# Two-level products in source order on every engine, sums two steps ahead, norms and side jobs cut into parts

## Chip, cores and metric

One core of a Trainium2 chip runs the program. The metric is the device time of one execution in microseconds (us); the time before is 2263.17 us, the median of 3 runs (2262.73 to 2263.86).

## What is computed

All arrays are float32. x is 3327 x 512; adj is 3327 x 3327, padded to 26 tiles of 128 rows.

```python
h = relu(layernorm(x))
a = (h @ Wq.T + bq) @ (h @ Wk.T + bk).T / sqrt(512) + adj + adj
x1 = x + softmax(a) @ (h @ Wv.T + bv)               # layer 0
h1 = relu(layernorm(x1))
A2 = adj + I;  d = diagonal(A2) ** -0.5
temp = A2 @ h1 @ W.T
out = x1 + relu((d * A2 * d.T) @ temp)              # layer 1
```

Three products have a 3327 x 3327 matrix on the left: exp(scores) with h (called g0 here), A2 with h1 (g1), and A2 with the scaled temp (g2). They are the "two-level products".

## The kernel before

**Scores.** The first part projects h and makes the exponentials of the scores in 52 pairs of row tiles, in a scheme with seven products in place of eight. It ends with pair 51. Each pair stores its exponentials and their sums to DRAM (`pd`), and sums of the adjacency (`sumd`: S3, S1, S2, S4 of each tile, of which the scores write S3 and S1). The matmuls are on L435, the accumulation of the row totals on L483, its last matmul against a column of ones on L490 (`total`), the sum S4 on L472 (`s4`, into a two-slot tile `mid 12` that is allocated anew for every two pairs).

**Steps of a product.** Each g runs seven sub-products (ORDER = p5, p1, p6, p7, p2, p3, p4). Each of these runs over two column strips s (896 and 768 columns, so moving operands of 448 and 384) and in each strip over seven steps t: six steps of two row tiles and a last one, t = None, of one tile. Hence 14 steps a sub-product, 98 a g, 294 in all; `number_of(g, r, s, t)` counts them. A step loads its left tile (`left`, two DMAs into one of five slots of `a_ring`, L658, L661 or L665; where the tile lies on the diagonal a VectorE add, L668, puts in the 1), forms four sums on VectorE (`four_sums`, L171 to L173, into one of three slots of `o_ring3`), and multiplies (L744: seven products, two matmul instructions each, into seven PSUM banks). The step t = None multiplies without sums (L736: four products, into the banks of p2, p3, p4 and into p8's).

**Right sides.** `Right` holds the eight 128 x 128 blocks of one step's right side: rows of h, h1 or temp from DRAM (`rowd`, L685), sometimes with more rows in `r_ring`, then one to two subtractions or additions and `four_differences` (L177 to L180) in `make`. A right side is made once and used in both strips.

**Gather.** After t = None, `gather` takes the seven banks and p8 apart: a ScalarE copy (L778), eight VectorE operations that read PSUM (L779 to L788), and `settle`, which adds into the result tiles `cts` (L767 to L774; two operations of full width, for p7 six, for p5 and p1 none). The next step's matmuls reuse the banks one by one, p1, p6, p7, p5, p2, p3, p4.

**Between the steps.** A table `between` places further work after steps: loads and makes of right sides; `Job`s, which add two adjacency tiles to S1 in turn and so write S2 and S4 for g1 (L808 to L820); and, as soon as rows of a result are complete, `attend` (g0: four products against the weights on L827 into bank p8, VectorE operations L842 and L843, the layer norm, a ScalarE Relu L847 and stores of x1 and h1), `temp` (g1: the same matmuls, a ScalarE multiplication L854, a store) and `finish` (g2: transposes L866 into bank p8, ScalarE L868, VectorE L869, the store of the output). There are 26 rows of each. `attend` and `temp` do 17 in the last sub-products of their g and 9 in the first of the next (every second step from step 0 of it, so one of the nine falls behind a t = None); two steps of each g's last strip hold two rows. `finish` stays in g2.

**What sets the order.** The scheduler of the framework orders the instructions of each engine by itself and may put later ones earlier; each engine's queue then runs in the order so fixed. Only the scores are held to source order, by the helper `in_order`, which chains each named engine's instructions. In the products the source places load two and sums one step ahead of the multiplication.

Of the kernel before, what the change touches and what calls it, by code (L numbers as in the profile page):

```python
# [15 lines left out]
P = 128  # L16
# [28 lines left out]
def graph_layers_kernel(  # L45
# [142 lines left out]
    def norm(src):  # L188

        st = small.tile([P, 6], F32, name="st")  # L190
        nc.vector.bn_stats(st, src)
        mv = small.tile([P, 2], F32, name="mv")
        nc.vector.bn_aggr(mv, st)
        ve = small.tile([P, 1], F32, name="ve")
        nc.vector.tensor_scalar(ve, mv[:, 1:2], EPS, None, op0=ALU.add)
        rstd = small.tile([P, 1], F32, name="rstd")
        nc.gpsimd.tensor_tensor(rstd, ve, mhalf, op=ALU.pow)
        nb = small.tile([P, 1], F32, name="nb")
        nc.vector.scalar_tensor_tensor(nb, mv[:, 0:1], -1.0, rstd, op0=ALU.mult, op1=ALU.mult)
        return rstd, nb  # L200
# [102 lines left out]
    def h_transposed(k):  # L303

        a, n = PACKS[k]
        for _, i in (o for o in order if o[0] == k):
            xt = first.pop(i) if i in first else load_x(i)
            rstd, nb = norm(xt)
            ht = n_ring([P, D], "ht")
            nc.scalar.activation(ht, xt, AF.Relu, bias=nb, scale=rstd)  # L310
            nc.gpsimd.dma_start(rowd[0][i], ht)
            pt = tp_bank("tp").rearrange("p (c e) -> p c e", c=DC)
            for c in range(DC):
                nc.tensor.transpose(pt[:, c], ht[:, c * P : (c + 1) * P], ident)
            w = slice((i % HALF - a) * P, (i % HALF - a + 1) * P)
            if i < HALF:
                nc.scalar.copy(hp[k][:, 0:2, :, w], pt.rearrange("p (a c) e -> p a c e", a=2))
            else:
                nc.scalar.copy(hp[k][:, 2, :, w], pt[:, 2:4])
                nc.vector.tensor_add(hp[k][:, 3, :, w], hp[k][:, 2, :, w], pt[:, 0:2])  # L320
                nc.vector.tensor_add(hp[k][:, 5, :, w], hp[k][:, 0, :, w], pt[:, 0:2])
        nc.vector.tensor_add(hp[k][:, 4], hp[k][:, 3], hp[k][:, 0])
        nc.vector.tensor_add(hp[k][:, 6], hp[k][:, 1], hp[k][:, 4])
# [78 lines left out]
    class Pair:  # L402
# [65 lines left out]
        def s4(self):  # L468
            if self.t % 2 == 0:
                Pair.fours = mid(12, [P, 2, Q[0]], "s4")  # L470
            self.last = Pair.fours[:, self.t % 2, : self.wd]
            nc.vector.tensor_add(self.last, self.e[:, 1], self.g[1][:, 0])  # L472
            nc.gpsimd.dma_start(self.to(pd)[:, 6], self.last)  # L473
# [11 lines left out]
        def total(self, m):  # L485

            if self.t < HALF - 1:
                return
            acc, ps = Pair.acc, tp_bank("tot")
            nc.tensor.matmul(ps[:1, : self.wd], ones, acc[:, m], start=True, stop=True)  # L490
            if m == 0:
                Pair.second = ps
                return
            lower, upper = acc[:1, 0], acc[:1, 1]
            nc.vector.tensor_copy(upper, Pair.second[:1, : self.wd])
            nc.vector.tensor_sub(lower, ps[:1, : self.wd], upper)
            c0 = STRIPS[self.s] * P
            dst = totd[:, c0 : c0 + 2 * H[self.s]].rearrange("o (y w) -> o y w", y=2)
            nc.gpsimd.dma_start(dst[:, :, self.c : self.c + self.wd], acc[:1])


    pairs = {}
    steps = [(n, t) for n in range(len(groups)) for t in range(HALF)]
# [32 lines left out]
    with in_order(*(e.engine for e in (nc.vector, nc.tensor, nc.gpsimd, nc.sync))):  # L536
# [14 lines left out]
        for what in (*beside[5:], *beside_of(k + 1)):  # L551
            what()
    nc.sync.dma_start(tot, totd[0].rearrange("(i p) -> p i", p=P))
# [5 lines left out]
    def seven():  # L559
        return {r: bank(ROLE[r], r) for r in ("p1", "p6", "p7", "p5", "p2", "p3", "p4")}  # L560

    def judge():
# [16 lines left out]
        one = small.tile([1, 4], F32, name="one")  # L579
# [17 lines left out]

    def prepare():
        wv_w1.append(weights(wvT))
        nc.vector.reciprocal(rs, tot)  # L600
        LD = adjT.shape[1]
        dg = const.tile([P, NT], F32, name="dg")
        with nc.allow_non_contiguous_dma(reason="the diagonal, once"):
            nc.sync.dma_start(dg, bass.AP(tensor=adjT.tensor, offset=adjT.offset, ap=[[LD + 1, P], [P * (LD + 1), NT]]))
        mh = const.tile([P, NT], F32, name="mh")
        nc.vector.memset(mh, -0.5)
# [23 lines left out]
    b_ring = ring(*((half, k) for k in (0, 1, 2, 3, 8, 9, 10, 11)))  # L630
# [12 lines left out]
    job_ring = ring(*spare[3:], (half, 14))  # L643
# [103 lines left out]
    def gather(ct, r, s, ps):  # L747
# [41 lines left out]
        if r == "p4" and s == 1:  # L789
            settle(hi)  # L790
        else:
            settle(slice(0, hw))
# [6 lines left out]
    class Job:  # L799


        def __init__(self, s, j):
            self.s, self.j = s, j

        def load(self):
            s, j, w, c0 = self.s, self.j, H[self.s], STRIPS[self.s] * P
            self.s1, *self.a = (job_ring([P, H[0]], "job")[:, :w] for _ in range(3))
            nc.gpsimd.dma_start(self.s1, sumd[s][j][:, 1])  # L808
            for k in range(2):
                r0 = (k * HALF + j) * P  # L810
                nc.gpsimd.dma_start(self.a[k], adjT[r0 : r0 + P, c0 : c0 + w])

        def make(self):
            before = self.s1
            for k, a in enumerate(self.a):
                tc.keep_in_program_order(nc.vector.tensor_add(a, a, before))  # L816
                d = diagonal(a, (k * HALF + self.j) * P, STRIPS[self.s] * P)
                if d:
                    nc.vector.tensor_add(a[:, d[0]], a[:, d[0]], d[1])
                nc.gpsimd.dma_start(sumd[self.s][self.j][:, 2 + k], a)  # L820
                before = a
# [8 lines left out]
    attended = []  # L830

    def attend(i):

        if not attended:
            bv_sb = mid(12, [P, D], "bv_sb")
            nc.sync.dma_start(bv_sb, bass.AP(tensor=bv.tensor, offset=bv.offset, ap=[[0, P], [1, D]]))
            attended.append(bv_sb)
        xt = view(2, 1).rearrange("p a w -> p (a w)")[:, len(attended) % 3 * D :][:, :D]
        attended.append(i)
        nc.sync.dma_start(xt, x[i * P : (i + 1) * P])  # L840
        ps = times_weights(i, wv_w1[0])
        nc.vector.scalar_tensor_tensor(xt, ps, rs[:, i : i + 1], xt, op0=ALU.mult, op1=ALU.add)  # L842
        nc.vector.tensor_add(xt, xt, attended[0])  # L843
        nc.gpsimd.dma_start(x1d[i], xt)
        rstd, nb = norm(xt)
        h1 = h_ring([P, D], "h1")
        nc.scalar.activation(h1, xt, AF.Relu, bias=nb, scale=rstd)  # L847
        nc.gpsimd.dma_start(rowd[1][i], h1)

# [6 lines left out]

    def finish(i, z=(0, 1), spot=None):
# [4 lines left out]
        xr = (xr_ring if spot is None else xr_last)([P, D], "xr")  # L862
        nc.sync.dma_start(xr[:, c0:c1], x1d[i][:, c0:c1])
# [21 lines left out]
    for g in range(3):  # L885
        for n, r in enumerate(ORDER):
            for t, e in enumerate(every):
                k = number_of(g, n, 0, t)
                rh = rights[g, r, e]
                lead = 3 if n == 0 else 7  # L890
                for what, when in ((rh.load, k - lead), (rh.make, k - 2 if n == 0 else k - 4)):
# [5 lines left out]
    for g, what in ((0, attend), (1, temp), (2, finish)):  # L897
        for t, i in {2: 0, 3: 1, 4: 2, 5: 3}.items():
            at(number_of(g, 5, 1, t), what, i)
        for t, i in enumerate((4, 5, 6, 14, 15, 16)):  # L900
            at(number_of(g, 6, 0, t), what, i)
        for t, its in {1: (7,), 2: (8, 9), 3: (10,), 4: (11, 12), 5: (13,)}.items():
            for i in its:
                at(number_of(g, 6, 1, t), what, i)
        if g < 2:
            for k, i in enumerate((*range(20, 26), *range(17, 20))):
                at(number_of(g + 1, 0, 0, 0) + 2 * k, what, i)
    for t, i in enumerate((17, 18, 19)):
        at(number_of(2, 6, 1, t), finish, i)
    for t, i in enumerate(range(20, NT)):  # L910
        at(number_of(2, 4, 0, t), finish, i, (1,))
    at(number_of(0, 0, 0, 1), prepare)
    at(number_of(0, 0, 1, 1), judge)
    at(number_of(1, 1, 0, 4), other_weights)

    jobs = [Job(s, j) for s in range(2) for j in range(HALF)]
    k0, k1 = number_of(0, 0, 0, 4), number_of(1, 1, 1, 2)
    for n, job in enumerate(jobs):
        k = k0 + n * (k1 - k0) // len(jobs)
        at(k, job.load)  # L920
        at(k + 3, job.make)

    for k in range(2):
        steps[k].load()
    for what in early:
        what()
    steps[0].sums()
    for k, step in enumerate(steps):
        if k + 2 < len(steps):
            steps[k + 2].load()  # L930
        if k + 1 < len(steps):
            steps[k + 1].sums()
        if step.t == 0:
            ps = seven()
        if not cts:
            set_up()
        if step.t is None:
            ps["p8"] = bank(ROLE["p8"], "p8")
        step.multiply(ps)
        if step.t is None:  # L940
            gather(cts[step.s], step.r, step.s, ps)
        for what, args in between.get(k, ()):
            what(*args)
    for n, i in enumerate(range(20, NT)):
# [378 lines left out]
```

## Time and profile before

The profiled execution took 2255.93 us, its span is 2254.1 us.

| view | reading |
|---|---|
| profiled execution / span | 2255.93 us / 2254.1 us |
| median of the timed runs | 2263.17 us |
| VectorE busy in the span | 1587.6 us (70%), 3095 instructions |
| ScalarE busy | 231.8 us (10%), 336 instructions |
| GpSimd busy | 391.4 us (17%), 629 instructions |
| DMA, mean over the span | 254 GB/s, 572.58 MB |
| 14 matmuls L744 undisturbed (chain of work) | 5.26 us with 448 columns, 4.51 us with 384 |
| 8 matmuls L827 undisturbed (chain of work) | 3.43 us |
| left tiles, issue to landing, median | 3.5 to 6.3 us |
| rows for right sides, issue to landing, median | 3.9 and 4.3 us |

A busy time is the union of an engine's instructions; matmul records overlap, so their mean duration (514 ns on L744) is longer than their distance. The idle time behind the bar of a group is what the engine stood still directly before its instructions, with the instruction that ended it. "SPq" is the queue of SyncE, which issues DMAs in order and waits in front of one whose buffer is not free.

### The profile page before, as it was taken

Reading aid. Unit: us, or ns where it says so; the run is one execution under the profiler, and the core shown is the slowest. Engines: PE = TensorE matmul, PEld = TensorE weight load, DVE = VectorE, ACT = ScalarE, POOL = GpSimd, SP = SyncE. Lnnn points to the kernel's source line nnn. Section 1 sums busy time; section 2 is a strip of 40 time slices with the busy share of each in tenths; the row PEclk is TensorE's granted clock in tenths of the full one; section 3 lists DMA queues with packets and bytes.
Section 4 is the critical chain, followed back from the end, with each engine's and each line's share of the span. In section 5 each row is a group of like instructions: output and inputs, shape, how many; then the busy total and the mean of one; then the engine's idle time right before and its main releaser. Section 6 shows DMA issues by size and latency. Waiting matters only on the chain.

```text
span 2254.1 us, 20860 instructions
## 1 busy us (share of the span) xinstructions
PE 2185.9 (97%) x6252; PEld 1164.8 (52%) x6252; DVE 1587.6 (70%) x3095; ACT 231.8 (10%) x336; POOL 391.4 (17%) x629
## 2 busy tenths in 40 slices
PE   8999999999989998999989999999999999999997
PEld 5555555455545454554444455555545555555554
DVE  6369788788867667877666777777645447677675
ACT  5321211122100000000100000000000000000011
POOL 5233333333321111011232220000000000000001
PEclk9999999999999999999999999999999999999998
DMA  7568888889988889888687787666646558766685
GB/s 249 206 213 305 292 300 284 301 290 321 360 269 318 322 293 335 284 296 280 205 292 261 245 307 247 222 206 215 198 140 207 160 170 287 223 199 214 202 278 162
DMA packets 237546, 572.58 MB, mean 254 GB/s; under 512 B 34218, under 2 KB 105360, under 8 KB 237424
## 3 DMA queue, kind: packets, MB, share of 16 engines
q1 hardware_dynamic: 185344, 368.48, 50.8%
q0 software_dynamic: 51216, 201.11, 24.0%
q10 hardware_dynamic: 864, 1.57, 0.2%
q8 instruction: 51, 0.84, 0.2%
q14 instruction: 71, 0.58, 0.1%
HBM read 403.21 MB, written 167.85 MB: 253 GB/s over the span
## 4 chain that ended last, share of the span: by engine, by line
PE 64%; issue 16%; POOL 7%; DMA 7%; DVE 3%; ACT 0%; SPq 0%; POOLq 0%; DVEq 0%
PE p L744 46%; PE p L827 6%; PE p L736 4%; DMA sum<-job 2%; PE Y L435 2%; PE Y L334 1%; POOL p L462 1%; POOL p L466 1%; POOL p L443 1%; POOL sum L427 1%; DMA job<-in_adjT_dram 1%; POOL p L473 1%; PE Z L435 1%; DMA rows<-row 1%; PE mm L288 1%
## 5 line engine op out<-in xcount | busy, mean ns | idle before, releaser
L744 PE MATMUL p<-part,b 128*128 128x448 f32 (+1 forms) x3528 | 1257.6, 514 | 13.5 <-DVE part L779 6.1
L744 PEld LDWEIGHTS p<-part,b 128*128 128x128 f32 x3528 | 668.7, 190 | 582.5 <-issue 318.7
L171 DVE TENSOR_TENSOR part<-part 128x896 f32<-128x896 f32 (+1 forms) x252 | 257.2, 1021 | 204.0 <-PE p L744 119.8
L435 PE MATMUL Y<-qt,hp 128*128 128x448 f32 (+1 forms) x832 | 309.0, 514 | 2.6 <-DVE g L439 1.6
L435 PEld LDWEIGHTS Y<-qt,hp 128*128 128x128 f32 x832 | 157.4, 190 | 138.0 <-issue 72.3
L435 PE MATMUL Z<-qt,hp 128*128 128x384 f32 (+1 forms) x416 | 162.6, 513 | 0.0
L827 PE MATMUL p<-w,ct 128*128 128x512 f32 x272 | 130.0, 619 | 13.4 <-DVE part L842 13.4
L173 DVE TENSOR_TENSOR part<-part,part 128x448 f32<-128x448 f32 (+1 forms) x219 | 128.7, 588 | 12.7
L736 PE MATMUL p<-part,b 128*128 128x448 f32 (+1 forms) x336 | 125.0, 513 | 6.6 <-DVE part L842 3.4
L172 DVE TENSOR_TENSOR part<-part,part 128x448 f32<-128x448 f32 (+1 forms) x219 | 128.6, 587 | 3.6
L435 PEld LDWEIGHTS Z<-qt,hp 128*128 128x128 f32 x416 | 78.8, 190 | 67.4 <-issue 36.2
L439 DVE SCALAR_TENSOR_TENSOR g<-g,Y 128x384 f32<-128x384 f32 (+1 forms) x156 | 91.4, 586 | 26.9 <-PE Y L435 25.1
L855 POOL DMA_DIRECT2D row<-ts x26 | 14.1, 542 | 467.3 <-ACT ts L854 467.3
L736 PEld LDWEIGHTS p<-part,b 128*128 128x128 f32 x336 | 63.3, 190 | 61.5 <-issue 32.7
L827 PEld LDWEIGHTS p<-w,ct 128*128 128x128 f32 x272 | 53.7, 199 | 76.9 <-issue 54.1
L778 ACT COPY part<-p 128x384 f32<-128x384 f32 (+1 forms) x33 | 16.5, 501 | 686.0 <-PE p L744 685.9
L435 PE MATMUL X<-qt,hp 128*128 128x384 f32 (+1 forms) x208 | 81.1, 512 | 0.0
L442 ACT ACTIVATE g<-g 128x768 f32<-128x768 f32 (+1 forms) x48 | 43.0, 896 | 352.5 <-DVE g L439 301.8
L427 POOL DMA_DIRECT2D sum<-o x52 | 37.0, 711 | 217.3 <-DVE o L421 151.6
L89 POOL DMA_DIRECT2D out_dram<-r x34 | 18.4, 543 | 308.9 <-DVE r L869 304.5
L816 DVE TENSOR_TENSOR job<-job 128x896 f32<-128x896 f32 (+1 forms) x52 | 53.0, 1020 | 23.5 <-DMA job<-in_adjT_dram 23.3
L177 DVE TENSOR_TENSOR b<-b 128x128 f32<-128x128 f32 x126 | 36.1, 287 | 46.9 <-DMA b<-row 38.3
(159 smaller groups left out, 1911.3 us busy)
## 6 DMA issues: line engine op xcount, KB each, us to landing
part<-sum SPq DMA_DIRECT2D x104, 448.0 KB, 4.7
part<-p SPq DMA_DIRECT2D x91, 448.0 KB, 6.3
part<-sum SPq DMA_DIRECT2D x104, 384.0 KB, 3.5
part<-p SPq DMA_DIRECT2D x91, 384.0 KB, 4.3
part<-in_adjT_dram SPq DMA_DIRECT2D x78, 448.0 KB, 4.4
b<-row SPq DMA_DIRECT2D x234, 128.0 KB, 3.9
part<-in_adjT_dram SPq DMA_DIRECT2D x78, 384.0 KB, 3.7
g<-in_adjT_dram SPq DMA_DIRECT2D x52, 448.0 KB, 4.5
```

The lines of the kernel that those rows point to most:

```text
L171: nc.vector.tensor_add(o[:, 0:2], g[:, 0:4:3], g[:, 1:2].to_broadcast([P, 2, g.shape[-1]]))
L172: nc.vector.tensor_add(o[:, 2], o[:, 1], g[:, 0])
L173: nc.vector.tensor_add(o[:, 3], o[:, 2], g[:, 2])
L177: yield nc.vector.tensor_sub(b[4], b[0], b[1])
L427: nc.gpsimd.dma_start(self.to(sumd)[:, 0:2], self.o)
L435: nc.tensor.matmul(ps[:, :wd], h_of(self.t, name, k), qt[B[name]][:, k], start=start and k == 0, stop=k == 1, skip_group_check=True)
L439: nc.vector.scalar_tensor_tensor(a[n], a[n], 2.0, ps[:, :wd], op0=ALU.mult, op1=ALU.add if sign > 0 else ALU.subtract)
L442: nc.scalar.activation(g[1], g[1], AF.Exp, **({"bias": pad} if self.t == HALF - 1 else {}))
L736: nc.tensor.matmul(ps[("p2", "p3", "p4", "p8")[k]][:, :w], b[:, z], a[:, 0, y], start=k == 3, stop=True)
L744: nc.tensor.matmul(ps[r][:, :w], b[:, i], m, start=self.t == 0, stop=self.t == PAIRS - 1 and r in ("p1", "p5", "p6", "p7"))
L816: tc.keep_in_program_order(nc.vector.tensor_add(a, a, before))
L827: nc.tensor.matmul(ps, cts[s][y][d][:, k * P : (k + 1) * P], w[d], start=d == 0, stop=d == DC - 1)
```

## The change

1. **Order.** All steps before the last strip of the last sub-product (`last = number_of(2, 6, 1, 0)`) are traced inside `in_order` for VectorE, TensorE, GpSimd, ScalarE and SyncE. The rest is left to the scheduler as before.
2. **Leads.** Left tiles are loaded three steps ahead (was two), sums formed two steps ahead (was one). Right sides are loaded 5 and made 3 steps ahead (was 7 and 4), those of p5 in g1 and g2 3 and 2 as before. `gather` returns its last `settle`, which runs behind the sums.
3. **attend in parts.** One step ahead `attend_load` loads x, at its step `attend` multiplies, adds and takes the statistics, one step later `attended` forms the bias, the Relu and the store. x (g0) and x1 (g2, `finish_load`) are loaded from ScalarE's queue instead of SyncE's.
4. **Jobs.** 52 jobs of one sum each (two loads, one addition, one store, two of four slots) in place of 26 jobs of two sums (three loads, two additions, two stores, three slots). Their loads go from GpSimd's queue to SyncE's. They lie between steps 7 and 164 (were 4 and 121). The second job of a tile reads the first one's result from DRAM.
5. **Totals and one-time work.** The last totals move from the end of the scores to step 1 and use bank p8 one after the other; `s4` keeps one tile for all pairs; bv has a slot of its own, which leaves seven slots for right sides (were eight); `prepare` and `judge` are cut in two and placed at steps 2, 6, 8 and 9.

```diff
         rstd = small.tile([P, 1], F32, name="rstd")
         nc.gpsimd.tensor_tensor(rstd, ve, mhalf, op=ALU.pow)
-        nb = small.tile([P, 1], F32, name="nb")
-        nc.vector.scalar_tensor_tensor(nb, mv[:, 0:1], -1.0, rstd, op0=ALU.mult, op1=ALU.mult)
-        return rstd, nb
+        def bias():
+            nb = small.tile([P, 1], F32, name="nb")
+            nc.vector.scalar_tensor_tensor(nb, mv[:, 0:1], -1.0, rstd, op0=ALU.mult, op1=ALU.mult)
+            return nb
+        return rstd, bias
...
         def s4(self):
-            if self.t % 2 == 0:
-                Pair.fours = mid(12, [P, 2, Q[0]], "s4")
-            self.last = Pair.fours[:, self.t % 2, : self.wd]
+            self.last = fours[:, self.t % 2, : self.wd]
...
+    def totals():
+        for m in range(2):
+            pairs[len(steps_of_scores) - 1].total(m, bank(ROLE["p8"], "tot"))
+        nc.sync.dma_start(tot, totd[0].rearrange("(i p) -> p i", p=P))
...
-    b_ring = ring(*((half, k) for k in (0, 1, 2, 3, 8, 9, 10, 11)))
+    b_ring = ring(*((half, k) for k in (0, 1, 2, 3, 8, 9, 10)))
...
-    job_ring = ring(*spare[3:], (half, 14))
+    job_ring = ring(*spare[2:], (half, 14))
...
-        if r == "p4" and s == 1:
-            settle(hi)
-        else:
-            settle(slice(0, hw))
+        return lambda: settle(hi if r == "p4" and s == 1 else slice(0, hw))
...
         def load(self):
-            s, j, w, c0 = self.s, self.j, H[self.s], STRIPS[self.s] * P
-            self.s1, *self.a = (job_ring([P, H[0]], "job")[:, :w] for _ in range(3))
-            nc.gpsimd.dma_start(self.s1, sumd[s][j][:, 1])
-            for k in range(2):
-                r0 = (k * HALF + j) * P
-                nc.gpsimd.dma_start(self.a[k], adjT[r0 : r0 + P, c0 : c0 + w])
+            s, j, w = self.s, self.j, H[self.s]
+            self.a, self.b = (job_ring([P, H[0]], "job")[:, :w] for _ in range(2))
+            r0, c0 = (self.k * HALF + j) * P, STRIPS[s] * P
+            nc.sync.dma_start(self.a, sumd[s][j][:, 1 + self.k])
+            nc.sync.dma_start(self.b, adjT[r0 : r0 + P, c0 : c0 + w])
...
+    def attend_load(i):
+        xts[i] = view(2, 1).rearrange("p a w -> p (a w)")[:, len(xts) % 3 * D :][:, :D]
+        nc.scalar.dma_start(xts[i], x[i * P : (i + 1) * P])
...
-        rstd, nb = norm(xt)
+        normed[i] = norm(xt)
+    def attended(i):
         h1 = h_ring([P, D], "h1")
-        nc.scalar.activation(h1, xt, AF.Relu, bias=nb, scale=rstd)
+        nc.scalar.activation(h1, xts[i], AF.Relu, bias=normed[i][1](), scale=normed[i][0])
         nc.gpsimd.dma_start(rowd[1][i], h1)
...
-                lead = 3 if n == 0 else 7
-                for what, when in ((rh.load, k - lead), (rh.make, k - 2 if n == 0 else k - 4)):
+                lead, make = (3, 2) if g and n == 0 else (5, 3)
+                for what, when in ((rh.load, k - lead), (rh.make, k - make)):
...
+    jobs = [Job(k, s, j) for k in range(2) for s in range(2) for j in range(HALF)]
+    k0, k1 = number_of(0, 0, 1, 0), number_of(1, 5, 0, 0) - 4
     for n, job in enumerate(jobs):
         k = k0 + n * (k1 - k0) // len(jobs)
         at(k, job.load)
-        at(k + 3, job.make)
+        at(k + 2, job.make)
+    def rows(g, k, i, *z):
+        if g == 0:
+            at(k - 1, attend_load, i)
+            at(k, attend, i)
+            at(k + 1, attended, i)
+        elif g == 1:
+            at(k, temp, i)
+        else:
+            at(k - 1, finish_load, i, *z)
+            at(k, finish, i, *z)
...
+    def run(k):
+        step = steps[k]
+        if k + 3 < len(steps):
+            steps[k + 3].load()
+        if step.t == 0:
+            banks_of.update(seven())
...
+        step.multiply(banks_of)
+        rest = gather(cts[step.s], step.r, step.s, banks_of) if step.t is None else None
+        if k + 2 < len(steps):
+            steps[k + 2].sums()
+        if rest:
+            rest()
+        for what, args in between.get(k, ()):
+            what(*args)
+    last = number_of(2, 6, 1, 0)
+    with in_order(*(e.engine for e in (nc.vector, nc.tensor, nc.gpsimd, nc.scalar, nc.sync))):
+        for k in range(last):
+            run(k)
+    for k in range(last, len(steps)):
+        run(k)
```

## The prediction

> **What bounds it now.** I began with the page's first part: the span, and how much of it each engine works.
>
> ```profile
> span 2254.1 us, 20860 instructions
> ...
> PE 2185.9 (97%) x6252; PEld 1164.8 (52%) x6252; DVE 1587.6 (70%) x3095; ACT 231.8 (10%) x336; POOL 391.4 (17%) x629
> ```
>
> TensorE bounds it, and no matmul goes away, so all there is to gain lies in its idle time and in matmuls that run below full rate. The second view was busy time by stretches: scores, g0, g1, g2 (columns: stretch, length, busy of each engine with instructions, clock, DMA share, GB/s).
>
> ```profile
> 0.00:638.00 638.00, 625.18 (x1856) 338.83 (x1857) 494.03 (x1011) 150.44 (x207) 223.36 (x333) 1.00 0.81 284
> 638.00:1201.50 563.50, 526.65 (x1438) 273.13 (x1437) 404.55 (x781) 22.49 (x33) 97.13 (x170) 0.97 0.83 288
> 1201.50:1745.70 544.20, 540.98 (x1498) 284.84 (x1497) 357.96 (x688) 26.65 (x41) 43.78 (x76) 1.00 0.68 224
> 1745.70:2241.30 495.60, 493.11 (x1465) 268.05 (x1463) 329.43 (x613) 31.27 (x53) 23.41 (x44) 1.00 0.68 214
> ```
>
> g0 is idle for 36.9 us, and its granted clock is 0.97. Against full rate: 14 matmuls L744 take 5.26 or 4.51 us, 8 of L827 3.43 (chain of work), 8 of L736 3.01 or 2.58 (start to next start in the timeline). A product is 7 x (6 x 5.26 + 3.01 + 6 x 4.51 + 2.58) = 449.5 us. g0 adds 17 attends (58.3) and 3 us of score, total and judge matmuls: 510.8, so it loses 52.7. g1 adds 26 times 3.43: 538.7, loses 5.5. g2 adds 9 temps and 104 transposes 0.109 apart: 491.7, loses 3.9. **All that the change can reach is 62.1 us.** The third view, waits of TensorE (us, times, longest), names the enders:
>
> ```profile
> PE p L827 <- DVE part L842: 13.4, 4, 6.0
> ...
> PE p L744 <- DVE part L779: 6.1, 2, 5.3
> PE tot L490 <- DVE acc L483: 5.8, 1, 5.8
> ...
> PE p L736 <- DMA part<-in_adjT_dram: 3.2, 1, 3.2
> PE p L744 <- DVE ct L779: 2.9, 1, 2.9
> ```
>
> VectorE frees PSUM too late, though it is busy for 404 of 563 us. The timeline says why; brackets hold the idle time before a line and what ended it:
>
> ```profile
> 651.30 0.56 DVE L472 TENSOR_TENSOR s<-e,g 128x384 f32<-128x384 f32 x1 [5.32 <-DMA p<-s]
> ...
> 852.59 0.69 DVE L712 TENSOR_TENSOR b<-b,rows 128x512 f32<-128x512 f32 x1 [3.38 <-DMA b<-row]
> ...
> 1163.75 5.40 PE L827 MATMUL p<-w,ct 128*128 128x512 f32 x8 [2.91 <-DVE part L842]
> ...
> 1176.51 0.69 DVE L706 TENSOR_TENSOR b<-rows 128x512 f32<-128x512 f32 x1 [6.57 <-DMA rows<-row]
> ...
> 1184.40 5.49 PE L827 MATMUL p<-w,ct 128*128 128x512 f32 x8 [6.01 <-DVE part L842]
> ```
>
> A `make` that the scheduler pulled forward waits for its rows at the head of VectorE's queue; L842, or the gather (L779), stands behind it, and TensorE behind that. After such a wait the 8 matmuls take 5.4 us, not 3.43: each long wait costs 2 more. After waits of 1.9 and less nothing like it follows.
>
> **What the change removes.** In source order nothing is pulled forward. `make` comes two steps (9 us or more) behind its load, whose rows land in 3.9 to 4.3. The slot of the right side is free by then with seven slots too: its last use is step k - 7, the load is at k - 5. A left tile's load waits for step k - 2 of the five slots; it is issued about four step times (20 us) before its matmuls and two before its sums, and lands in 3.5 to 6.3. So the waits on rows go, and with them nearly all of the 52.7 and 5.5; what follows is what is late next.
>
> **What stays or comes, term by term.**
>
> *Boundary, 3.5 (8.7 now).* One tile for s4 ends the 5.32 us wait. The two totals now share bank p8, so the second waits for the copy of the first (0.58 by L495, and about 0.2 to start) behind a `make` (1.8); with 1.0 left of the scores' own waits I take 3.5. Ends: 1.8 with the copy alone, 8.7 if VectorE's backlog is as long as the old wait.
>
> *Six gathers of p7, 5.* In source order VectorE does eight operations (0.62), the next sums (1.09 + 2 x 0.62), six settles (1.0 apart), then the sums after them. Counted from the start of t = None: the last bank read ends at 3.8, sums 6.0, settles 12.1, of the sums after them the one that TensorE uses first 13.8; TensorE wants it at 12.7. That is 1.1 for strip 0, by the same count 0.2 for strip 1, and 1 more where a job (1.02) falls between. Three times, with some jobs: 5. Ends: 0, as g1 and g2 show now, and 12. Other gathers fit.
>
> *Four gathers with an attend just ahead, 8.9.* L842 (0.75), L843, the statistics and two small operations hold VectorE for 2.5 us when t = None starts, and eight reads and the sums then end near 10. TensorE waits 0.3 to 1.2 for banks and 0.4 to 1.7 for sums or a right side; behind p3's strip 1 the backlog (settle 1.8, make 1.7, job 1.0, sums 2.3, make 1.7) brings L842 to 19.8 where the next attend wants the bank at 16.9: 3.0. Sum 3.3 + 1.5 + 2.9 + 1.2. Ends: 0 if VectorE catches up, 18 if each grows past 3 and the slow matmuls follow.
>
> *Two rows in one step, 3.7.* Now four L744 matmuls lie between the pair (seen at 1712.37). Held to source order TensorE waits for L842 (0.75) or L854 (0.69) and 0.2 to start: 4 x 0.93. Ends 2.9 and 8.
>
> *A row behind t = None, 1.8.* Twice, 0.9 until the last gather read frees p8. Ends 0 and 3.
>
> *First finish in p2 of g2, 5.6 (1.6 now).* Its transpose needs p7's last settle, which the sums (2.4) now precede: TensorE is ready at 7.8, the settle ends at 11.5, and 3.6 us of wait bring 2 of slow matmuls. Ends 1.5 and 8.
>
> *Tail, 2.3.* Not in source order; as now.
>
> Sum 30.8; gain 62.1 - 30.8 = 31.3.
>
> **At nothing.** ScalarE takes 26 loads of x and 32 of x1, each 0.43 to issue (the first x loads on its queue): 25 us on an engine that is busy for 80 of the products' 1603. Behind a load that waits there stands the gather's copy L778; its slot was stored two steps before. SyncE takes 104 job loads, 0.33 to 0.45 each, 41 us over 157 steps; with the rest it issues for under 2 us in each step of 4.5 to 5.3. The 26 loads more are 11 MB, beside 288 GB/s in g0. Dependent VectorE operations now follow each other 0.72 apart instead of 0.53: 2 us more per strip of 34.5, where VectorE works 24 to 31.5. If that cover goes, p6 in g0 (31.5) is first to wait. The 26 norms in parts take GpSimd's power (idle 22.9 us in all on L199) off VectorE's queue. In some strips of g1 and g2 the diagonal's add (L668) for step k + 3 now heads VectorE's queue in step k; its tile was issued a step time (4.5 to 5.3) before and lands in 3.7 to 4.4, and at 8 us it would still be inside the sums' lead. In the scores, a copy three times waits some 0.3 for its matmul: VectorE has room.
>
> SyncE's queue shows the load of x at work: the x load is held from 1280.70 to 1287.37, and the left tile behind it lands late, the 3.2 us wait of L736 above.
>
> ```profile
> 1280.28 0.42 SPq L665 DMA_DIRECT2D part<-in_adjT_dram  x1
> 1287.37 0.33 SPq L840 DMA_DIRECT2D part<-in_x_dram  x1
> ...
> 1288.70 6.00 SPq L665 DMA_DIRECT2D part<-in_adjT_dram  x3
> ```
>
> By this row ScalarE's queue is worth g1's loss, 3.2 and the slow matmuls after it, and I keep it in the gain. The Trainium skill speaks against it: "DMA: Bandwidth & Descriptors", section "Issuing engines are not separate DMA queues", says that all engines' DMAs run on the same 16 DMA engines, so that another issuing engine saves only issue time. By that rule this part is worth nothing and the time would be 5 higher, 2237.
>
> **Rivals.**
>
> *B, half comes back: 2248.* Held to source order, TensorE has no filler, and VectorE's backlogs behind gathers with attends reach their upper end: that term at 18 and the boundary at 8.7, p7 at 7. That is 16 more. For it: the 3.0 above stands at the edge. Against it: two steps of lead on the sums.
>
> *C, slower: 2284.* The jobs' wait for slots moves to SyncE, ahead of every left tile. Now GpSimd waits for it: "POOL job L811 <- DMA sum<-job: 117.1, 44, 7.2". Two jobs now fit into the slots, and a job's store is issued four steps before its slot is wanted, so I count no wait. If stores came so late that SyncE stood past the 10 us by which a tile precedes its sums, each us beyond would cost 52 jobs x 1 = 52 us; from 0.6 us on the whole is slower than before. At 1 us: 2232 + 52 = 2284.
>
> *D, no effect: 2262.* The scheduler's order is near source order where nothing is late (g1 and g2 lose 9.4 in 1040 us). If the waits of g0 come from transfers that are late in any order, they return. Against it: the waits end at DMAs whose loads were issued just before.
>
> **The numbers.** Chances: forecast 0.62, B 0.19, C 0.11, D 0.08. The profiled execution takes 2255.93 (span 2254.1 and 1.8 around it), so 2224.6 by the sum; the median of the timed runs is 7.2 higher, a difference that I carry over: 2231.9, **2232**. All terms at their lower ends leave 8.5 (1.8 + 2.9 + 1.5 + 2.3), a time of 2209.6; all at their upper ends 60, a time of 2261. The range 2209 to 2264 holds the forecast, B and D, and leaves C out. The measurement can tell some 0.2% (4.5 us) from no change: faster 0.81 (forecast and B), same 0.07, slower 0.12 (C and a part of D).
>
> **What would show it.** g0 should take about 526 us in place of 563.5 with a clock near 1.00, g1 545, g2 502. TensorE's waits for L842 should shrink to four of some 1 us and one of 3; none should be ended by rows. New are a wait of L490 for L495, and one of 3 to 4 us of L866 for L771. SyncE's waits should be for TensorE (slots), not for stores of x1 or jobs. It is wrong if VectorE waits for left tiles at L171 or L668 step after step, or if SyncE waits for `sum<-job`.

## The result, and the profile after

The changed kernel takes **2241.0 us** (median of 4 runs, 2238.1 to 2246.1) against 2263.5 us (4 runs): a ratio of 0.9898, 95% interval 0.9874 to 0.9922, a gain of 22.5 us. The forecast was 2232, a gain of 31.3. Its profiled execution took 2241.45 us. The first part of its page (the span, then busy time and share of each engine):

```profile
span 2239.3 us, 20973 instructions
...
PE 2184.3 (98%) x6252; PEld 1165.8 (52%) x6252; DVE 1623.1 (72%) x3095; ACT 230.9 (10%) x336; POOL 357.4 (16%) x555
```

The same matmuls in a shorter span. Busy time by stretches, from the first product on (scores, g0, g1, g2; the columns as before):

```profile
0.00:644.20 644.20, 629.30 (x1856) 342.23 (x1857) 494.23 (x1011) 150.53 (x207) 218.89 (x333) 0.99 0.79 278
644.20:1169.80 525.60, 517.46 (x1438) 272.10 (x1437) 397.15 (x731) 22.05 (x33) 65.22 (x97) 0.99 0.84 293
1169.80:1722.00 552.20, 542.85 (x1498) 283.79 (x1497) 379.80 (x705) 26.46 (x41) 46.27 (x76) 1.00 0.75 254
1722.00:2223.60 501.60, 494.72 (x1465) 267.69 (x1463) 350.52 (x648) 30.92 (x53) 23.31 (x44) 1.00 0.67 219
```

| stretch | before | forecast | after |
|---|---|---|---|
| g0 | 563.5 | 526 | 525.6 |
| g1 | 544.2 | 545 | 552.2 |
| g2 | 495.6 | 502 | 501.6 |

g0 and g2 are as forecast to half a us; g1 is 7.2 longer than forecast. The products begin 6.2 us later than before, and 2.9 are lost behind the last work; both come back below. TensorE's longest waits in the products (us in total, times, longest):

```profile
PE p L838 <- DVE ct L806: 6.0, 2, 5.3
PE p L762 <- DVE part L172: 4.9, 4, 1.9
PE p L838 <- DVE part L850: 3.9, 3, 2.2
...
PE pt L884 <- DVE part L789: 3.1, 2, 2.5
PE p L838 <- ACT ts L866: 1.7, 2, 0.8
```

(L838 is L827 of before, L850 is L842, L806 is L788, L762 is L744, L884 is L866, L866 is L854.) The four waits of L827 of up to 6.0 us for L842 have become three of up to 2.2. VectorE's waits between 640 and 1300 us say why: of those that ended at rows for a right side (50.6 us before, on L177, L178, L706, L708 and L712) one is left.

```profile
DVE b L724 <- DMA rows<-row: 2.3, 1, 2.3
```

The longest wait in the products is new: 5.3 us at a row behind t = None. It can be followed in the timeline of g1's first strip (start, duration, engine, line; ACTq is ScalarE's queue of DMA issues; matmul rows left out in between):

```profile
1206.80 0.81 ACT L857 ACTIVATE h<-part,nb,rstd 128x512 f32<-128x512 f32 x1 [10.36 <-DVE nb L201]
1206.88 0.33 ACTq L845 DMA_DIRECT2D part<-in_x_dram  x1
...
1210.46 0.75 DVE L850 SCALAR_TENSOR_TENSOR part<-p,rs,part 128x512 f32<-128x512 f32 x1 [2.41 <-DMA part<-in_x_dram]
...
1215.30 0.81 ACT L857 ACTIVATE h<-part,nb,rstd 128x512 f32<-128x512 f32 x1 [7.68 <-DVE nb L201]
...
1216.01 0.51 ACT L796 COPY ct<-p 128x448 f32<-128x448 f32 x1
...
1216.56 0.62 DVE L797 TENSOR_TENSOR ct<-p,ct 128x448 f32<-128x448 f32 x1 [1.35 <-ACT ct L796]
...
1221.27 5.08 PE L838 MATMUL p<-w,part 128*128 128x512 f32 x8 [5.31 <-DVE ct L806]
```

ScalarE, now in source order, holds the load of the next row's x behind a Relu (L857) that waits for VectorE. The x lands late and VectorE waits 2.41; the next Relu comes late, and the gather's copy (L796) stands behind it. The whole gather, and the row that needs bank p8, are late by that.

### The profile page after: what moved, and what is told of

It reads as the page before. It is cut to its first block, busy times and chain, and to the rows that moved or that the text cites. A ratio compares the mean times of both kernels' runs of the same rounds, so it can differ in the third digit from the quotient of the medians.

```text
span 2239.3 us, 20973 instructions
## 1 busy us (share of the span) xinstructions
PE 2184.3 (98%) x6252; PEld 1165.8 (52%) x6252; DVE 1623.1 (72%) x3095; ACT 230.9 (10%) x336; POOL 357.4 (16%) x555
## 5 line engine op out<-in xcount | busy, mean ns | idle before, releaser
L762 PE MATMUL p<-part,b 128*128 128x448 f32 (+1 forms) x3528 | 1254.8, 514 | 6.5 <-DVE part L172 4.9
L762 PEld LDWEIGHTS p<-part,b 128*128 128x128 f32 x3528 | 667.6, 190 | 573.8 <-issue 300.8
L171 DVE TENSOR_TENSOR part<-part 128x896 f32<-128x896 f32 (+1 forms) x252 | 256.6, 1018 | 87.9 <-PE p L762 41.7
L172 DVE TENSOR_TENSOR part<-part,part 128x448 f32<-128x448 f32 (+1 forms) x219 | 129.4, 591 | 7.3
L838 PE MATMUL p<-w,ct 128*128 128x512 f32 x272 | 125.5, 601 | 5.6 <-DVE part L850 3.9
L443 DVE SCALAR_TENSOR_TENSOR g<-g,Y 128x384 f32<-128x384 f32 (+1 forms) x156 | 91.3, 585 | 26.8 <-PE Y L439 25.3
L832 POOL DMA_DIRECT2D sum<-job x52 | 28.5, 548 | 487.3 <-DVE job L829 269.5
L797 DVE TENSOR_TENSOR part<-p,part 128x384 f32<-128x384 f32 (+1 forms) x33 | 19.3, 585 | 104.7 <-ACT part L796 57.3
L838 PEld LDWEIGHTS p<-w,ct 128*128 128x128 f32 x272 | 51.8, 192 | 67.5 <-issue 52.0
L796 ACT COPY part<-p 128x384 f32<-128x384 f32 (+1 forms) x33 | 16.5, 500 | 669.5 <-PE p L762 639.3
L838 PE MATMUL p<-w,part 128*128 128x512 f32 x144 | 67.3, 604 | 6.0 <-DVE ct L806 6.0
```

The costliest lines, as they stand in the source:

```text
L171: nc.vector.tensor_add(o[:, 0:2], g[:, 0:4:3], g[:, 1:2].to_broadcast([P, 2, g.shape[-1]]))
L172: nc.vector.tensor_add(o[:, 2], o[:, 1], g[:, 0])
L443: nc.vector.scalar_tensor_tensor(a[n], a[n], 2.0, ps[:, :wd], op0=ALU.mult, op1=ALU.add if sign > 0 else ALU.subtract)
L762: nc.tensor.matmul(ps[r][:, :w], b[:, i], m, start=self.t == 0, stop=self.t == PAIRS - 1 and r in ("p1", "p5", "p6", "p7"))
L797: nc.vector.tensor_sub(c22, p["p6"], c11)
L832: nc.gpsimd.dma_start(sumd[self.s][self.j][:, 2 + self.k], self.a)
```

## Experiments

Losses are the distance between starts of matmuls beyond the undisturbed one; "product time" runs from the first product to the start of the last one in the profiled execution (before 1599.5, after 1575.7). The letters S, T, N and so on are the theories named in the expectations. Runs of one kernel spread by some 2 to 9 us (after: 2238.1 to 2246.1), so where two kernels differ by less than about 5 us the median alone does not tell them apart.

| kernel | us | ratio to before, 95% | product time |
|---|---|---|---|
| after, no order in the products | 2286.2 | 1.0083 to 1.0137 | 1620.5 |
| before, order on five engines | 2317.0 | 1.0218 to 1.0262 | 1661.0 |
| before, order on VectorE alone | 2245.8 | 0.9903 to 0.9943 | 1590.8 |
| after, order on VectorE alone | 2210.0 | 0.9744 to 0.9784 | 1547.6 |
| after, order on VectorE and TensorE | 2227.8 | 0.9828 to 0.9874 | 1565.8 |
| after, order on all but TensorE | 2214.2 | 0.9771 to 0.9811 | 1550.6 |
| after, x and x1 on SyncE | 2235.8 | 0.9859 to 0.9898 | 1569.8 |
| order on VectorE alone, x and x1 on SyncE | 2211.1 | 0.9753 to 0.9786 | 1548.0 |
| after, sums one step ahead | 2281.0 | 1.0059 to 1.0099 | 1623.7 |
| order on VectorE alone, sums one step ahead | 2215.4 | 0.9776 to 0.9823 | 1553.4 |
| after, norm in one piece | 2244.9 | 0.9908 to 0.9941 | 1581.9 |
| after, rows off t = None, x two steps ahead | 2233.4 | 0.9857 to 0.9890 | 1567.3 |

**The new parts without the order.**

```diff
-    with in_order(*(e.engine for e in (nc.vector, nc.tensor, nc.gpsimd, nc.scalar, nc.sync))):
-        for k in range(last):
-            run(k)
+    for k in range(last):
+        run(k)
```

> The changed kernel with all its leads, parts and queues, but with the products left to the scheduler's order again. Theory (source order brings the gain, because no make of a right side is run ahead of its rows on VectorE): the waits on rows at the head of VectorE's queue come back, the products lose about 55 to 65 us instead of 38, and the time is 2256 to 2268. Rival 'leads' (the earlier loads and sums bring it, whatever the order): 2236 to 2246, as changed. Rival 'queue' (the x loads off SyncE's queue bring it): also 2236 to 2246.

Measured 2286.2: 23 slower than before, worse than expected. VectorE's timeline at the first gather:

```profile
687.05 1.09 DVE L829 TENSOR_TENSOR job<-job 128x896 f32<-128x896 f32 x1 [2.72 <-DMA job<-sum]
688.17 0.29 DVE L831 TENSOR_TENSOR job<-job,ident 128x128 f32<-128x128 f32 x1
688.38 0.62 DVE L797 TENSOR_TENSOR ct<-p,ct 128x448 f32<-128x448 f32 x1
```

A job's addition waits for its load at the head of VectorE's queue, and the gather (L797), on which TensorE waits 7.1 us, stands behind it. Such waits come to 39.3 us, and VectorE's waits for rows, the theory's own, are back with 37.8 us between 640 and 1300 us. The scheduler pulls all 52 jobs into g0, which loses 77 us; g1, with no job left, loses 0.9. So the new parts need the order, and what they need it for is VectorE's queue.

**The order without the new parts**: the kernel before, its step loop put into the same `in_order` for five engines.

> The kernel before with nothing but source order on the five engines for the same steps; loads two and sums one ahead, norms whole, x on SyncE, two-sum jobs on GpSimd. Theory: the waits on rows go, but whole norms hold VectorE for GpSimd's power (about 0.9 in each of 26) and sums one ahead leave the gathers bare; half to two thirds of the gain, 2245 to 2256. Rival 'leads': order without the leads is worth nothing or costs, 2262 to 2290. Rival 'queue': x loads in order on SyncE hold the left tiles behind them, 2262 or more.

Measured 2317.0, 54 slower than before; this part of the theory fell. TensorE waits 43.6 us in 23 places for the sums' second operation L172. One of them in the timeline:

```profile
895.18 1.09 DVE L771 TENSOR_TENSOR ct<-ct,ct 128x896 f32<-128x896 f32 x1
896.19 0.95 DVE L171 TENSOR_TENSOR part<-part 128x768 f32<-128x768 f32 x1
897.18 0.56 DVE L172 TENSOR_TENSOR part<-part,part 128x384 f32<-128x384 f32 x1
...
897.79 2.92 PE L744 MATMUL p<-part,b 128*128 128x384 f32 x4 [3.53 <-DVE part L172]
```

The sums of the second step after the gather begin when the last settle (L771) ends: held to source order they can't pass it, and one step ahead is too late.

**The order on VectorE alone.**

```diff
-    with in_order(*(e.engine for e in (nc.vector, nc.tensor, nc.gpsimd, nc.scalar, nc.sync))):
+    with in_order(*(e.engine for e in (nc.vector,))):
```

> The changed kernel with only VectorE chained to source order; TensorE, GpSimd, ScalarE and SyncE are left to the scheduler. Theory (VectorE's order carries it): 2236 to 2246, as changed; the pairs of rows in one step may get their filler matmuls back, 4 us in the best case. Rival (the order of the loads on SyncE carries it): about half the gain or less, 2250 to 2265.

Measured **2210.0**, 31 faster than the change and 53 faster than before: the best version. VectorE's and GpSimd's instructions stand in the same order as in after; TensorE's, ScalarE's and SyncE's differ. So GpSimd's chain changes no order, and the other three together cost 31 us. Which, was the question of the next two.

**The order on VectorE and TensorE; on all but TensorE** (the same line, with the engines named).

> The changed kernel with the source order kept on VectorE and TensorE alone. With VectorE alone it took 2210.0 us, with all five 2241.0: 31 us are lost by the four other chains. Theory T: TensorE's chain loses them, since a free order let it put products of the next step between a step and the rows behind it, and after a gather first those sub-products whose operand was there: then this is 2232 to 2246, and its stalls are at the second row of a step (1.0 each), behind p7's gathers (1.2 to 2.1) and ahead of the rows at the boundary of the groups. Rival A: ScalarE's chain loses them, since it puts the gather's copy behind a Relu that waits for VectorE: then this is 2208 to 2218.

> The changed kernel with the source order kept on VectorE, GpSimd, ScalarE and SyncE, and free on TensorE. Theory T (TensorE's chain loses the 31 us): 2208 to 2218, with no stall at second rows and behind p7's gathers. Rival A (ScalarE's or SyncE's chain loses them): 2228 to 2241, with the copy of the gather after p5's strip behind a Relu and a wait of some 5 us at the row behind it. Both in part: 2218 to 2228.

Measured 2227.8 and 2214.2. TensorE's chain costs 17.8 where it is added to VectorE's, and 26.8 where it is the last to be added (2241.0 - 2214.2); the three others cost 4.3 without it and 13.2 with it. T is the larger cause, but 2227.8 lies below its range and above A's: neither chain carries the 31 alone, and 8.9 us arise only where TensorE's chain and the others meet (31.0 - 17.8 - 4.3). The place where two rows share a step, in after:

```profile
1130.83 3.60 PE L838 MATMUL p<-w,ct 128*128 128x512 f32 x8
1135.27 3.70 PE L838 MATMUL p<-w,ct 128*128 128x512 f32 x8 [0.84 <-DVE part L850]
```

and the same rows with the order on VectorE alone:

```profile
1118.26 3.60 PE L838 MATMUL p<-w,ct 128*128 128x512 f32 x8
1121.69 1.45 PE L762 MATMUL p<-part,b 128*128 128x384 f32 x4
1122.98 3.60 PE L838 MATMUL p<-w,ct 128*128 128x512 f32 x8
```

Four matmuls of the next step fill the time in which VectorE empties the bank. Behind p7's gather, where VectorE's operations are the same in both, after shows

```profile
886.73 0.95 DVE L829 TENSOR_TENSOR job<-job 128x768 f32<-128x768 f32 x1
887.59 0.95 DVE L171 TENSOR_TENSOR part<-part 128x768 f32<-128x768 f32 x1
888.58 0.56 DVE L172 TENSOR_TENSOR part<-part,part 128x384 f32<-128x384 f32 x1
889.19 3.22 PE L762 MATMUL p<-part,b 128*128 128x384 f32 x5 [1.93 <-DVE part L172]
```

and the free TensorE 45 matmuls without a gap:

```profile
873.45 14.98 PE L762 MATMUL p<-part,b 128*128 128x384 f32 x45
```

The late sum is ready no earlier there (L172 ends at 885.16 us, some 2.7 us after that step's first matmul), so TensorE must take the products first whose left operand is not that sum.

**The order on VectorE alone, for the kernel before.**

> The kernel before with nothing but the source order on VectorE in the products. With the order on all five engines it was 2317.0, 54 us over before, and in its trace the step after most gathers waits 2 to 5 us for the second step's sums (L172), which stand behind the whole gather on VectorE. Theory S: these sums are the cause, and TensorE's freedom can't hide them, since all its products of that step need them: 2275 to 2305. Rival T: TensorE's chain is the cause there too: 2225 to 2250.

Measured 2245.8: a gain of 16.5 against before, where five chains lose 54. S falls: TensorE's freedom hides most of the late sums (its waits for L172 fall from 43.6 to 7.2 us). Of the change's 22.5 us, most can be had by one chain on the old parts.

**The sums one step ahead, under five chains and under VectorE's alone.**

```diff
+        if k + 1 < len(steps):
+            steps[k + 1].sums()
         if step.t == 0:
...
-        if k + 2 < len(steps):
-            steps[k + 2].sums()
         if rest:
```

> The changed kernel with the sums one step ahead of their products, ahead of the step, as in the kernel before; everything else stays. Theory S: two steps ahead, between the halves of the gather, is what makes the order bearable; without it the waits for L172 that the order alone showed in the second step after a gather come back, some 19 of 1 to 5 us, 45 us in all there: 2265 to 2290. Rival L: the leads of the makes and the jobs in parts do that, and the place of the sums is worth little: 2238 to 2250.

> The changed kernel with the source order on VectorE alone and the sums one step ahead. Under all five chains that step cost 40 us (2281.0 against 2241.0). Theory F: a free TensorE hides about half of such a wait, as it did for the kernel before (2245.8 with VectorE's order against 2317.0 with all five): 2222 to 2240, with waits for L172 behind the gathers that are shorter than 2 us. Rival S: the wait is one for operands that all products need, and comes back whole: 2245 to 2255.

Measured 2281.0 and 2215.4. Under five chains the earlier sums are worth 40 us, as S says; under VectorE's chain alone 5.4, less than F expected. The two steps of lead mostly pay for the chain on TensorE.

**x and x1 on SyncE**, under five chains and under VectorE's alone.

```diff
-        nc.scalar.dma_start(xts[i], x[i * P : (i + 1) * P])
+        nc.sync.dma_start(xts[i], x[i * P : (i + 1) * P])
...
-        nc.scalar.dma_start(xrs[i][:, c0:c1], x1d[i][:, c0:c1])
+        nc.sync.dma_start(xrs[i][:, c0:c1], x1d[i][:, c0:c1])
```

> The changed kernel with the loads of x and x1 on SyncE's queue in place of ScalarE's. Theory: the load is placed a step ahead in source order and its slot was freed two steps before, so SyncE hardly waits; 0 to +3, 2239 to 2246, and perhaps a little faster in g1's first strip, where ScalarE's x load now stands behind a late Relu. Rival 'queue' (moving x off SyncE carries the gain): +8 to +20, 2249 to 2261.

> The changed kernel with the source order on VectorE alone and with x and x1 loaded by SyncE. With VectorE alone it took 2210.0; with SyncE's loads under all five chains 5 us less than the changed kernel. Theory H: those 5 us were the x load that stood behind a Relu in ScalarE's fixed order; with ScalarE free there is nothing left to win: 2207 to 2213. Rival Q: issuing on ScalarE costs in itself: 2202 to 2206.

Measured 2235.8 and 2211.1. Under five chains SyncE's queue is 5.2 better (its slowest run is 0.5 below the fastest of after), and the loss in g1's first strip falls from 8.1 to 3.3 us; with ScalarE free it makes no difference. H holds: it is the place behind the Relu, not the issuing.

**The rows off t = None.** The load of x goes two steps ahead, the rows of the next product move one step off t = None, and the second layer's weights load later.

```diff
-            at(k - 1, attend_load, i)
+            at(k - 2, attend_load, i)
...
-                rows(g, number_of(g + 1, 0, 0, 0) + 2 * k, i)
+                rows(g, number_of(g + 1, 0, 0, 0) + 2 * k + (k > 2) + (k > 5), i)
...
-    at(number_of(1, 1, 0, 4), other_weights)
+    at(number_of(1, 1, 1, 0), other_weights)
```

> The changed kernel with the x loads of the rows issued two steps ahead, and the rows of the next product moved one step off the place behind a gather's corner products (t = None) in p5 and p1. Theory R: the row behind t = None is the mis-sized term; in the profile of after it cost 5.5 us of waiting and 1.9 of a slower clock in the second group and 0.9 in the third, where 0.9 each were forecast: without it 2231 to 2236. Rival V: VectorE is busy 43.7 of 56.4 us in that strip and is the bound there wherever the row stands: 2237 to 2243.

With three x tiles the h1 of rows 7 to 10 is made from the x of rows 10 to 13, so the output of this kernel is wrong and only its time is of use. The amount of work is the same, and the four rows lie in g0, which takes as long as in after (525.7 against 525.6). Measured 2233.4, 7.6 less, as R says; the three edits were not tried apart. g1 takes the 545 us of the forecast:

```profile
1169.20:1714.10 544.90, 540.93 (x1497) 283.51 (x1497) 378.50 (x703) 26.22 (x41) 48.02 (x76) 1.00 0.75 257
```

**The norm in one piece**: `attended(i)` follows at the end of `attend`.

> The changed kernel with the norm of an attended row in one piece again: the bias (nb) follows on VectorE right behind the power on GpSimd. Theory N: with VectorE in source order each of the 26 rows then waits some 1.5 us for the power (L195's end at 1202.66 us to L197's end at 1204.10 us in one row of after), 39 us of VectorE time; the six strips with rows have some 80 us in which VectorE is idle, so a part reaches TensorE: 2247 to 2265. Rival L: the idle time takes in all of it: 2239 to 2245.

Measured 2244.9: at the upper end of L's range, just below N's. A wait for the power that ends at 1051.49 us takes 0.74, half of N's price. But four times TensorE waits for the gather's copy (L796), 10.1 us in all: the Relu, which now waits for this row's own norm, stands directly ahead of the copy on ScalarE (L858 at 1051.74, L796 at 1052.46, TensorE at 1052.97 after 3.11). So a part does reach TensorE, as N says, though by another way. At the medians it is worth 3.9 us, which the spread of the runs does not separate (2242.1 to 2246.7 against 2238.1 to 2246.1); the product times differ by 6.2.

## Why the prediction was right, and where it was not

**Right: the mechanism, and g0.** `make`s pulled ahead of their rows were what held VectorE, and source order on VectorE takes these waits away: with VectorE's chain alone the kernel before has none of them left between 640 and 1300 us, where it had 50.6 us. That the other four chains would cost time the prediction priced only in part, as told below. The terms, worked out anew from the losses of the trace after (its three stretches lose 38.2 in all; what the terms leave is spread over small waits):

| term | forecast | after |
|---|---|---|
| boundary | 3.5 | 2.7 |
| gathers of p7 | 5 | 7.8 |
| gathers behind an attend | 8.9 | 6.6 |
| two rows in one step | 3.7 | 4.4 |
| a row behind t = None | 1.8 | 7.9 |
| first finish | 5.6 | 3.5 |
| tail of the products | 2.3 | 3.1 |
| sum | 30.8 | 36.0 |

**The step that failed is "A row behind t = None, 1.8"**, with ends 0 and 3; it took 7.9. It counted VectorE's reads of p8 from a gather that starts on time. The gather started late. The longer of its two waits is 5.3 us in after, 2.6 with x on SyncE, and 1.1 with ScalarE and SyncE out of the chains. So about half of it was the load of x that stood behind a Relu, another 1.5 goes where these two queues are free (in after the gather's copy stood behind the next Relu), and the rest is near the 0.9 that the prediction had counted. The prediction saw that queue ("Behind a load that waits there stands the gather's copy L778"), but asked whether the load's slot was free, not what the load stood behind. Moving these rows and loading x a step earlier brought 7.6 of the 9.0 us between forecast and time.

The other terms miss in both directions and in part cancel: the gathers of p7 took 2.8 more, the first finish 2.1 and the gathers behind an attend 2.3 less. The first finish was luck: its wait was followed by no slow matmuls (last section).

**Also wrong: "ScalarE's queue is worth g1's loss".** The 3.2 us wait of the left tile is gone, but it is gone with x on SyncE too, so the queue did not win it; and the same loads cost 5.2 more on ScalarE than on SyncE. The Trainium skill, "DMA: Bandwidth & Descriptors", section "Issuing engines are not separate DMA queues", promised nothing from another issuing engine but the issue time; with ScalarE free, 2210.0 against 2211.1 agrees with it.

**Priced too low: the missing filler.** Rival B named it ("TensorE has no filler"); the forecast charged it only at the double rows. There the 3.7 was close (4.4), but TensorE's chain costs 17.8 to 26.8 in all, since the waits behind p7's gathers and at the rows arise from it too. The time of 2241.0 lies about as near to B (2248) as to the forecast, but not by B's terms: the gathers behind an attend took 6.6 where B has 18, the boundary 2.7 where it has 8.7.

**Rival C** failed at its price. SyncE does wait for the jobs' stores, 36.0 us in 11 places, where "I count no wait" stood; with the order on VectorE alone it waits 178.5 us for them in 43 places, and that kernel is the fastest. "SyncE waits for `sum<-job`" was one of the prediction's signs of being wrong; it came, and the kernel is faster than before all the same. The other one, VectorE's waits for left tiles, did not come: on L171 and L686 (L668 of before) they fell from 107.3 us in 56 places to 76.7 in 30 between 638 and 2240 us. **D** is out: the waits on rows did not return.

**Outside the products.** The first score matmul starts at 120.8 us in the profile of before and at 125.4 in that of after, but in the eleven profiles with the new code it starts at 120.8 to 125.4 and in the three with the old code at 120.8 to 123.4, so 4.6 of the 6.2 us lie within what one and the same code varies. The 7.2 between the profile of before and its median, which the forecast carried over, is large enough to hold that. Behind the last store, the closing DRAIN on GpSimd's queue took 5.79 us in all eleven kernels with the new parts and 3.50 in all three with the old ones, so it belongs to the program; with the semaphore step ahead of it (1.60 against 1.03) that is the 2.9. Why, stays open.

**Open as well.** With VectorE's chain alone and sums one step ahead, the new parts still win 30 us over the old (2215.4 against 2245.8). In the old ones VectorE waits between 640 and 1300 us 30.5 us for the power on GpSimd (1.5 in the new), 9.7 for the totals, 7.7 for jobs and 5.2 for s4; which of these carries the 30 was not tried, nor how the 13.2 us of the other chains divide beyond the 5.2 of the x loads.

## What to carry to other kernels

In this kernel it paid to chain only the engine whose queue went wrong: VectorE, 2210.0 us, while chains on the four others took back 31 of a possible 53 us. An engine that is the bound gains from its freedom to fill a short wait with other ready work; a lead that looks essential (the sums, 40 us) may only be paying for that freedom. When a queue is put in source order, read for every instruction on it what stands directly ahead and whom that waits for, above all for loads and copies on an engine that is otherwise idle.

## What the hardware showed unexpectedly

The same wait has two prices. At the first finish TensorE waits 2.53 us in after and goes on at full rate (14 matmuls in 5.44):

```profile
2020.98 0.33 PE L884 MATMUL pt<-ident,part 128*128 128x128 f32 x1 [2.53 <-DVE part L789]
2021.15 5.44 PE L762 MATMUL p<-part,b 128*128 128x448 f32 x14
```

With x on SyncE it waits just as long, and the granted clock is 0.50 for the next 6 us:

```profile
2007.57 0.47 PE L884 MATMUL pt<-ident,part 128*128 128x128 f32 x1 [2.53 <-DVE part L789]
2007.84 8.33 PE L762 MATMUL p<-part,b 128*128 128x448 f32 x14
```

The prediction charged 2 us of slow matmuls to every long wait and none to waits of 1.9 us and less. The wait of 2.53 us costs nothing more or 2.9 more, and the wait of 1.93 us behind p7's gather in g0 was followed by 1.7 us of slow matmuls in after and by none with x on SyncE.

A grid in time decides. Nine of the fourteen traces have stretches of slow clock between 200 us and 60 us before the end, 52 in all, each at a granted clock of 0.50. All of them begin on a grid of 3.41 us, one for each trace (within 0.02 us), and last one to three units of it. Each began behind a unit in which TensorE, by its records, stood idle for at least 1.92 us, and no unit at full clock with more than 1.97 us idle was without that effect (the ends of matmuls are modelled, so these two bounds are estimates). In after the waits at the first finish fell across two units, with 1.5 and 1.6 us idle; with x on SyncE 2.4 us of them fell into one. A slow unit costs 1.7 us, half its length. So differences of 2 or 3 us between two kernels can be luck with that grid alone.

The Trainium skill, "TensorE: Matmul & The Clock Gate", "Part 1: The HAM clock gate", states that activity is judged in free-running windows of some 3.4 us, and the grid of 3.41 us agrees with it. It also puts the slow state behind at least one idle window of that length; here some 1.9 us of idle time inside one window was enough, and the measurement decides.
